# Softmax sums divided out by exp of a negated logarithm instead of a transfer, and the steps of a fused attention and mixture-of-experts kernel laid out anew

## The chip, the cores and the metric

The kernel runs on one core of a Trainium2 chip. The metric is the time of one execution on the device in microseconds, lower is better; the median of three executions is compared. The engines are named as in the profile: PE (TensorE, matmuls; PEld is its weight load), DVE (VectorE), ACT (ScalarE), POOL (GpSimd) and SP (SyncE, which here only issues DMAs).

## The reference

64 batches of 128 tokens with 128 features go through a gated cross-attention over a context of 77 tokens with 96 features per batch, then through a gated mixture of 8 experts of which each token takes the best two. All is float32. Cut to what matters:

```python
q = heads(layernorm(x) @ Wq)            # 16 heads of 8
k, v = heads(ctx @ Wk), heads(ctx @ Wv)
attn = softmax(where(mask, q @ k.T * 8 ** -0.5, -big))
x = x + tanh(g_xattn) * (unheads(attn @ v) @ Wo)

h = layernorm(x)
score, idx = top_k(softmax(h @ Wg), 2)
score = score / (score.sum(-1) + 1e-8)
y_e = (silu(h @ W11[e]) * (h @ W12[e])) @ W2[e]      # I = 256
x = x + tanh(g_ffn) * sum(score[k] * y_idx[k] for k in range(2))
```

## The kernel before

**Attention.** Four batches make a group; there are 16 groups (`G`, `NG`). One loop step `i` handles one batch in a pipeline: `scores` of batch i (four matmuls into the one PSUM tile `sc`, L843; then on DVE the maximum `mx`, L852, and the subtraction in two pieces, `pe` and `pls`, L855), `turn` of batch i-1 (PE turns the weights, `tp` L865, ACT takes the exponential into `pT`, L870), `values` of batch i+2 (`pv`, L818 and L828, then the ACT copy `va`, L834), `mix` of batch i-2 (`po`, L897, then the ACT copy `os`, L904) and `turn_last` of batch i-1 (`tl`, L878). The last product gives two things side by side: with `va` as weights the weighted values, and with `own`, a constant of zeros and ones, the sums of the softmax weights, in the same rows. So the quotient can be formed after `mix`.

`own` repeats each head's sum over the 8 rows of that head, but the sums then have 128 rows for 16 heads. Before, the step `sums` collects 16 rows of each of the four batches with four DMAs (`zc`, 8 KB each), `inverses` takes one DVE reciprocal over 64 x 128 (`rz`, L548) and spreads it back to 128 rows with four DMAs (`rb`, 64 KB each, L551), and `quotients` multiplies (`aT`, L560). `project` (`py`, L569) and `residual` (L575) follow, then the second layer norm and the routing.

**Order of the work.** All steps of a group that are not in the batch pipeline have a place in the table `AT`: `"sums": (6, POST)` puts it at loop step 4g+6, after the pipeline's work; `PRE` puts it ahead. The order of instructions on PE, ACT, DVE and POOL is exactly the order in which the program writes them; on SP the framework's scheduler sets it. Within one step and place, older groups come first. Each engine takes its queue in order, so an instruction that waits holds up all that stand behind it. Three PSUM buffers (`product`) are shared by `tp`, `tl`, `po` and all the steps' products.

**Routing.** For each group DVE finds the best two experts of a token (L629 to L664), POOL adds up counts (`both` L673, `run` L677), PE and DVE turn them to rows (`places`, `dest`), and POOL scatters the rows to a buffer in memory sorted by expert (`xg`, L707): one indirect DMA for each batch and each of the two choices, so eight per group, here as two in each of the four steps `dispatch0` to `dispatch3`, with a memset of one element between. The groups form two parts with a sorted buffer each; part 0 holds the first `SPLIT` = 11 groups. The steps that build the list of tiles (`tiles_*`) run once per part, and `bounds*` writes an empty block behind each expert's rows.

**Experts.** The sorted rows are worked off in tiles of 128, 142 in all, 95 of part 0 and 47 of part 1. A tile is loaded (`xt`), turned (`ptt` L972, `xTt` L974), goes up (`pu` L982, ACT silu L988, DVE product L990), is turned (`phh` L997, `hTt` L999), goes down (`pot` L1005, `y` L1011) and is scattered by POOL into token order (`yb`, L1012), in a pipeline of six further steps. The part of `AT` that lies past the attention loop, `rest`, is spread over the first tiles of part 0 less four. Results of part 0's groups are fetched (`ys`), added to x (`combine`, L1048) and stored, beginning 19 tile steps after part 0's tiles, two steps apart: at steps 114 to 140. The groups of part 1 follow after the last tile. The pool for `ys` has four buffers.

**Layer norm.** Its factor is ln and exp on ACT (`rs_a`, L346), or a power on POOL where `late` is set: before, for the second norm of the last three groups. ACT holds one function table at a time; the attention uses one with both exp and ln, loaded once at the start, while the experts' silu needs another.

Of the kernel before, what the change touches and what calls it, by code (L numbers as in the profile page):

```python
# [8 lines left out]
F32 = mybir.dt.float32  # L9
# [8 lines left out]
HEADS = 16  # L18
HD = 8
# [5 lines left out]
JL = 16  # L25
PRE, POST = 0, 1
TOPK = 2
LATE = 3
RW = 132
PAST = 1 << 20  # L30
LN_EPS = 1e-5
GATE_EPS = 1e-8
SPLIT = 11


@with_exitstack
def tile_gated_xattn_moe(
# [84 lines left out]
    nc.scalar.dma_start(out=wk, in_=Wk)  # L122
    nc.scalar.dma_start(out=wq, in_=Wq)
    nc.scalar.dma_start(out=wv, in_=Wv)
    nc.scalar.dma_start(out=wo_in, in_=Wo)
    nc.scalar.dma_start(out=wg, in_=Wg)
    nc.scalar.dma_start(out=gates[:, 0:1], in_=g_xattn.partition_broadcast(P))
    nc.scalar.dma_start(out=gates[:, 1:2], in_=g_ffn.partition_broadcast(P))
# [131 lines left out]
    nc.gpsimd.memset(own, 0.0)  # L260
    for k in range(2):
        nc.vector.tensor_copy(
            own[:, k, 2 * k : 2 * k + 2], h64.unsqueeze(2).to_broadcast([P, 2, HD])
        )
    nc.vector.tensor_copy(
        own[:, 2:4].rearrange("p u h d -> p (u h) d"),
        h16.rearrange("p u h -> p (u h)").unsqueeze(2).to_broadcast([P, 2 * HQ, HD]),
    )
    iota8 = const.tile([P, E], U32, name="iota8")
    nc.gpsimd.iota(iota8, [[1, E]], base=0, channel_multiplier=0)  # L270

# [3 lines left out]
    czs = [const.tile([CD, G, 3, JL], F32, name=f"czs{i}") for i in range(3)]  # L275
    for t in pls + czs:
        nc.gpsimd.memset(t, 0.0)
    spare_w = const.tile([1, 1], F32, name="spare_w")


    for pt in parts:
# [9 lines left out]
    with ExitStack() as ph:  # L291
# [76 lines left out]
        def transposed(src, n):  # L368
# [5 lines left out]
            nc.scalar.copy(xT, pt)  # L374
            return xT

        AT = {
            "loads": (-22, POST),  # L380
            "stats_a0": (-13, POST),
            "sel_0": (-13, POST),
            "stats_a1": (-9, PRE),
            "sel_1": (-11, PRE),
            "shift_a": (-8, POST),
            "sel_2": (-10, POST),
            "context_t": (-7, PRE),
            "rows_a0": (-8, POST),
            "rows_a1": (-6, PRE),
            "keys": (-2, PRE),  # L390
            "queries_t": (-6, POST),
            "queries": (-4, PRE),
            "sums": (6, POST),
            "inverses": (7, PRE),
            "quotients": (7, POST),
            "project": (8, POST),
            "residual": (8, POST),
            "stats_f0": (9, PRE),
            "stats_f1": (9, POST),
            "shift_f": (11, PRE),  # L400
            "rows_f0": (11, PRE),
            "rows_f1": (12, PRE),
            "rows_f2": (14, PRE),
            "rows_t": (12, POST),
            "logits": (14, PRE),
            "less_max": (14, PRE),
            "gates_exp": (16, PRE),
            "gates": (16, PRE),
            "experts": (16, PRE),
            "counts": (16, PRE),  # L410
            "places": (18, PRE),
            "places_in": (18, PRE),
            "tiles_count": (17, POST),
            "tiles_ends": (17, POST),
            "tiles_list": (18, PRE),
            "tiles_turn": (18, POST),
            "tiles_keep": (19, PRE),
            "dispatch0": (19, PRE),
            "dispatch1": (19, POST),
            "dispatch2": (20, POST),  # L420
            "dispatch3": (21, POST),
            "bounds0": (18, PRE),
            "bounds1": (19, PRE),
            "bounds2": (19, POST),
            "bounds3": (20, POST),
        }
        TURN = {}

# [104 lines left out]
            nc.scalar.copy(gr.qT, pq)  # L533

        @step("sums")
        def sums(gr, g):
            gr.zc = s2.tile([G * HEADS, S], F32, tag="zc", name=f"zc_{g}")
            for b in range(G):  # L540
                nc.sync.dma_start(
                    out=gr.zc[b * HEADS : (b + 1) * HEADS], in_=gr.os[0:P:HD, b, 1]
                )

        @step("inverses")
        def inverses(gr, g):
            rz = s2.tile([G * HEADS, S], F32, tag="rz", name=f"rz_{g}")
            nc.vector.reciprocal(rz, gr.zc)  # L548
            gr.rb = s2.tile([P, G, S], F32, tag="rb", name=f"rb_{g}")
            for b in range(G):  # L550
                nc.sync.dma_start(  # L551
                    out=gr.rb[:, b],
                    in_=rz[b * HEADS : (b + 1) * HEADS].unsqueeze(1)
                    .to_broadcast([HEADS, HD, S]),
                )

        @step("quotients")
        def quotients(gr, g):
            gr.aT = s2.tile([P, T], F32, tag="aT", name=f"aT_{g}")
            nc.vector.tensor_tensor(  # L560
                gr.aT.rearrange("p (b t) -> p b t", b=G), gr.os[:, :, 0], gr.rb, ALU.mult
            )


# [17 lines left out]
        @step("stats_f1")  # L582
        def stats_f1(gr, g):
            gr.ln.stats(2, 4)
            gr.ln.factors(late=g >= NG - LATE)

        @step("shift_f")
        def shift_f(gr, g):
# [112 lines left out]
            nc.vector.tensor_reduce(to, at, AX.X, ALU.add)  # L701
            nc.vector.tensor_copy(gr.dest, to)

        def dispatch(b):
            def f(gr, g):
                for k in range(TOPK):
                    i = nc.gpsimd.indirect_dma_start(  # L707
                        out=part_of(g).xg[:, :],
                        out_offset=bass.IndirectOffsetOnAxis(
                            ap=gr.dest[:, k, b : b + 1], axis=0  # L710
                        ),
                        in_=gr.rows[:, b, k, :],
                        in_offset=None,
                    )
                    apart(i, f"dispatch{part_of(g).c}")
                    nc.gpsimd.memset(spare_w, 0.0)

            return f

        for b in range(G):  # L720
            step(f"dispatch{b}")(dispatch(b))


        def of_part(name):
# [83 lines left out]
        def values(gr, g, b):  # L808


            pvm = pv[:, : 8 * 32].rearrange("p (q k m) -> p q k m", q=NQ, k=2)
            wvm = wv.rearrange("c (q k h d) -> c q k h d", q=NQ, k=2, h=2)
            pvl = pv[:, 8 * 32 : 12 * 32].rearrange("p (f u m) -> p f u m", f=2, u=2)
            wvl = wv.rearrange("c (f u h d) -> c f u h d", f=2, u=2, h=HQ)
            for h in range(2):
                for k in range(2):
                    o = 8 * (2 * k + h)
                    nc.tensor.matmul(  # L818
                        pvm[64 * h : 64 * h + 64, :, k, o : o + HD],
                        gr.cT[:, b, :JM], wvm[:, :, k, h], start=True, stop=True,  # L820
                    )
            cz = gr.cz[:, b].rearrange("c z j -> c (z j)")
            for z in range(2):
                for u in range(2):
                    for hp in range(2):
                        h = 2 * hp + z
                        r = 64 * u + 32 * hp
                        nc.tensor.matmul(  # L828
                            pvl[r : r + 32, :, u, h * HD : h * HD + HD],
                            cz[:, JL * (1 - z) : JL * (1 - z) + 32],  # L830
                            wvl[:, :, u, h], start=True, stop=True,
                        )
            va = a4.tile([P, 12, 32], F32, tag="va", name=f"va_{g}_{b}")
            nc.scalar.copy(va.rearrange("p u m -> p (u m)"), pv[:, : 12 * 32])  # L834
            return va
# [48 lines left out]
                pT[:, 8:10], tp, AF.Exp, bias=drop[:, 1, i : i + 1], scale=scale  # L884
            )

        def mix(b, va, pT, os, n):

            po = product([P, 2, S], f"po_{n}")
            for v in range(2):  # L890
                for c in range(3):
                    for q in range(NQ):
                        if v == 0:
                            w = va[:, 2 * q + c if c < 2 else 8 + q]
                        else:
                            w = own[:, c if c < 2 else 2 + q % 2].rearrange("p h d -> p (h d)")
                        nc.tensor.matmul(  # L897
                            po[32 * q : 32 * q + 32, v, :],
                            w,
                            pT[:, 2 * q + c if c < 2 else 8 + q // 2, :],  # L900
                            start=(c == 0),
                            stop=(c == 2),
                        )
            nc.scalar.copy(os[:, b], po)  # L904

# [10 lines left out]
        for i in range(min(TURN)[0], NBT + 2):  # L918
# [11 lines left out]
            if 0 <= i - 2 < NBT:  # L930
                g, b = divmod(i - 2, G)
                if b == 0:
                    groups[g].os = s3.tile([P, G, 2, S], F32, tag="os", name=f"os_{g}")
                mix(b, vas.pop(i - 2), pTs.pop(i - 2), groups[g].os, f"{g}_{b}")
            if 0 <= i - 1 < NBT:
                turn_last(pTs[i - 1], i - 1)
            advance(i, POST)
        advance(NBT + 2, PRE)
        advance(NBT + 2, POST)
        at_.close()  # L940


        lp = ph.enter_context(tc.tile_pool(name="lp", bufs=26))
# [57 lines left out]
        def down(ti, t):  # L1001
            po = ps_u.tile([P, D], F32, tag="pd", name=f"pot_{t}")
            for c in range(NC):
# [5 lines left out]
                )  # L1009
            y = yp.tile([P, D], F32, tag="y", name=f"y_{t}")  # L1010
            nc.vector.tensor_scalar_mul(y, po, ti.x[:, D + 1 : D + 2])  # L1011
            i = nc.gpsimd.indirect_dma_start(  # L1012
                out=ti.pt.yb[:, :],
                out_offset=bass.IndirectOffsetOnAxis(
# [5 lines left out]
                oob_is_err=False,  # L1020
            )
            apart(i, f"results{ti.pt.c}")
            nc.gpsimd.memset(spare_w, 0.0)


        ts = [Tile(pt, k) for pt in parts for k in range(pt.nt)]
# [89 lines left out]
```

## Time and profile before

| | us |
|---|---|
| three executions | 801.7, 793.98, 795.58 |
| median | 795.58 |
| the profiled execution | 799.03 |
| its span on the profile | 797.3 |
| PE busy | 665.8 (84%) |
| DVE busy | 484.1 (61%) |
| ACT busy | 388.8 (49%) |
| POOL busy | 363.3 (46%) |
| mean granted clock of PE | 0.936 |

The first scores start at about 30 us, the last group leaves the attention loop at about 447, the experts run from 451 to 776, and the last store ends at 797.3. A row of the groups gives the source line, engine, operation, what it writes and reads, and the count, then the busy time in us and the mean of one in ns, then how long the engine stood idle just before and what ended most of that. A row of the waits gives engine and tile waited for, then the total in us, the count, and the longest. A row of the timeline gives start, duration and the instruction, and in brackets how long its engine had been idle, with what released it. "Remote" is a release that the profile does not name.

### The profile page before, as it was taken

The numbers are of one execution on the slowest core, as the hardware profiler recorded it, in microseconds if no ns is written. First come the engines' busy times: TensorE is split into PE (matmuls) and PEld (weight loads), VectorE is DVE, ScalarE is ACT, GpSimd is POOL, SyncE is SP. The second block draws the span as 40 slices with busy tenths as digits, with TensorE's granted clock in tenths as the row PEclk, the third lists the DMA queues.
The fourth block names the chain that finished last, engine by engine and source line by source line (L and its number), as shares of the span: only waits on it lengthen the run. The fifth ranks groups of instructions, "written<-read, shape, count | busy, mean of one in ns | idle before, by whom it ended". The sixth has DMA issues, their size and how long they took to land.

```text
span 797.3 us, 21532 instructions
## 1 busy us (share of the span) xinstructions
PE 665.8 (84%) x7695; PEld 462.5 (58%) x7695; DVE 484.1 (61%) x1452; ACT 388.8 (49%) x960; POOL 363.3 (46%) x774
## 2 busy tenths in 40 slices
PE   2999999988998989887988758888788678998880
PEld 2577776766676666666656436555555445665450
DVE  4467888777877877775668434544444434556653
ACT  3577877656665667664554333234334223342230
POOL 4211113455345445543225435665666576565451
PEclk9999999999999999997989879898999899999995
DMA  6671111111111110110121342222222212446626
GB/s 155 180 186 28 28 23 36 35 47 38 46 35 48 33 36 28 38 37 19 34 57 34 71 92 60 65 69 58 67 76 62 78 55 71 115 153 195 173 68 202
DMA packets 75753, 58.40 MB, mean 73 GB/s; under 512 B 16075, under 2 KB 69471, under 8 KB 75648
## 3 DMA queue, kind: packets, MB, share of 16 engines
q1 hardware_dynamic: 57088, 35.27, 18.3%
q0 software_dynamic: 8640, 17.06, 6.6%
q10 hardware_dynamic: 9920, 4.69, 2.1%
q8 instruction: 63, 1.03, 0.5%
q14 instruction: 42, 0.34, 0.1%
HBM read 28.98 MB, written 24.20 MB: 67 GB/s over the span
## 4 chain that ended last, share of the span: by engine, by line
PE 71%; DVE 8%; issue 7%; DMA 4%; SPq 3%; ACT 3%; another core or an unknown queue 3%; POOL 1%; ACTq 0%; POOLq 0%; DVEq 0%
PE pu L982 15%; PE po L897 11%; PE tp L865 8%; PE pot L1005 7%; PE sc L843 6%; PE phh L997 4%; PE ptt L972 3%; PE tl L878 2%; PE pv L818 2%; PE py L569 2%; PE pq L531 2%; PE pg L622 2%; PE pv L828 2%; DMA rb<-rz 1%
## 5 line engine op out<-in xcount | busy, mean ns | idle before, releaser
L1012 POOL DMA_INDIRECT yb<-y,xt x142 | 140.7, 991 | 130.4 <-DVE xTt L974 69.3
L707 POOL DMA_INDIRECT xg<-rows,dest x128 | 125.1, 977 | 90.3 <-DVE gm L629 60.7
L982 PE MATMUL pu<-wx,xTt 128*128 x284 | 158.5, 641 | 7.8 <-issue 6.7
L988 ACT ACTIVATE sgt<-pu 128x256 f32<-128x256 f32 x142 | 54.5, 384 | 196.0 <-PE pu L982 122.3
L990 DVE TENSOR_TENSOR ht<-sgt,pu 128x256 f32<-128x256 f32 x142 | 59.6, 420 | 117.1 <-ACT sgt L988 65.9
L852 DVE TENSOR_REDUCE mx<-sc 128x16 f32<-128x1232 f32 x64 | 91.9, 1435 | 39.2 <-PE sc L843 35.2
L997 PEld LDWEIGHTS phh<-ident,ht 128*128 128x128 f32 x284 | 40.2, 146 | 94.7 <-issue 76.1
L870 ACT ACTIVATE pT<-tp,drop 128x512 f32<-128x512 f32 x128 | 82.0, 685 | 24.9 <-PE tp L865 16.9
L1005 PE MATMUL pot<-wx,hTt 128*128 x568 | 90.3, 284 | 0.1
L865 PEld LDWEIGHTS tp<-ident,pe 128*128 128x128 f32 x512 | 61.7, 153 | 32.8 <-issue 15.8
L865 PE MATMUL tp<-ident,pe 128*128 128x128 f32 x512 | 78.7, 302 | 2.0 <-ACT kb L520 1.3
L855 DVE TENSOR_TENSOR pe<-sc,mx 128x1024 f32<-128x1024 f32 x64 | 78.4, 1225 | 2.2
L1005 PEld LDWEIGHTS pot<-wx,hTt 128*128 128x128 f32 x568 | 78.3, 200 | 0.2 <-issue 0.2
L897 PE MATMUL po<-pT,own 128*32 128x128 f32 x1536 | 66.4, 278 | 10.7 <-issue 10.7
L972 PE MATMUL ptt<-ident,xt 128*128 128x128 f32 x142 | 42.7, 300 | 35.6 <-DVE xTt L974 22.1
L1011 DVE TENSOR_SCALAR y<-pot,xt 128x128 f32<-128x128 f32 x142 | 49.3, 347 | 31.8 <-remote 10.9
L997 PE MATMUL phh<-ident,ht 128*128 128x128 f32 x284 | 57.1, 284 | 12.5 <-ACT hTt L999 8.4
L897 PE MATMUL po<-pT,va 128*32 128x128 f32 x1536 | 61.5, 279 | 4.8 <-issue 4.1
L843 PE MATMUL sc<-kb,qT 32*128 32x308 f32 x512 | 59.0, 525 | 3.8 <-DVE pls L855 3.1
L999 ACT COPY hTt<-phh 128x256 f32<-128x256 f32 x142 | 52.3, 368 | 14.9 <-PE pu L982 8.6
L897 PEld LDWEIGHTS po<-pT,own 128*32 128x32 f32 x1536 | 48.2, 112 | 18.3 <-issue 17.9
L834 ACT COPY va<-pv 128x384 f32<-128x384 f32 x64 | 30.9, 483 | 53.5 <-PE po L897 23.3
(161 smaller groups left out, 1037.7 us busy)
## 6 DMA issues: line engine op xcount, KB each, us to landing
xt<-xg SPq DMA_DIRECT2D x142, 66.0 KB
ys<-yb SPq DMA_DIRECT2D x16, 512.0 KB
rb<-rz SPq DMA_DIRECT2D x64, 64.0 KB
out_dram<-x ACTq DMA_DIRECT2D x16, 256.0 KB
x<-in_x_dram SPq DMA_DIRECT2D x15, 256.0 KB
yb<-y,xt POOLq DMA_INDIRECT x142
wx<-in_L_ffn_W_dram SPq DMA_DIRECT2D x2, 1024.0 KB
xg<-rows,dest POOLq DMA_INDIRECT x128
```

The source lines that it names most:

```text
L707: i = nc.gpsimd.indirect_dma_start(out=part_of(g).xg[:, :], out_offset=bass.IndirectOffsetOnAxis(ap=gr.dest[:, k, b : b + 1], axis=0), in_ ...
L843: nc.tensor.matmul(sc[:, q, :W], gr.qT[r, b * S : (b + 1) * S], gr.kb[r, b].rearrange("p h j -> p (h j)"), start=True, stop=True,)
L852: nc.vector.tensor_reduce(mx[:, :, :, 0], sv, AX.X, ALU.max)
L855: nc.vector.tensor_tensor(dst[:, :, :, : j1 - j0], sv[:, :, :, j0:j1], mx.to_broadcast([P, NQ, HQ, j1 - j0]), ALU.subtract,)
L865: nc.tensor.transpose(tp[:, u, :], pe[:, q + u // 2, 2 * (u % 2) : 2 * (u % 2) + 2].rearrange("p h j -> p (h j)"), ident,)
L870: nc.scalar.activation(pT[:, 2 * q : 2 * q + 4], tp, AF.Exp, bias=drop[:, 0, i : i + 1], scale=scale)
L897: nc.tensor.matmul(po[32 * q : 32 * q + 32, v, :], w, pT[:, 2 * q + c if c < 2 else 8 + q // 2, :], start=(c == 0), stop=(c == 2),)
L972: nc.tensor.transpose(pt, ti.x[:, :D], ident)
L982: nc.tensor.matmul(pu.rearrange("p j i -> p (j i)"), ti.xT, wxf[:, bass.ds(ti.e, 2 * I)], start=True, stop=True,)
L997: nc.tensor.transpose(pt[:, c], ti.h[:, c], ident)
L1005: nc.tensor.matmul(po, ti.hT[:, c], wxf[:, bass.ds(ti.e + w, D)], start=(c == 0), stop=(c == NC - 1),)
L1012: i = nc.gpsimd.indirect_dma_start(out=ti.pt.yb[:, :], out_offset=bass.IndirectOffsetOnAxis(ap=ti.x[:, D : D + 1].bitcast(I32), axis=0), i ...
```

## The change

- `sums` and its transfers go. `mix` copies only the values to `os`, and ACT takes the logarithm of the sums into `lz`. `inverses` becomes one exponential of -`lz` on ACT, in place over the group's 128 x 512, and `quotients` multiplies by `lz`.
- In `values`, four tiles of 32 columns at 64 moving columns take the place of tiles of 64 columns at 32. The order of the heads inside 32 rows changes; `own` and the rows of `Wo` follow it, `Wo` now loaded in eight DMAs of 16 rows on ACT's queue.
- `dispatch` becomes eight steps of one scatter. The memset of `spare_w`, now 128 x 1, stands ahead of each scatter, also of the result scatters.
- `SPLIT` is 12: part 0 has 103 tiles, part 1 has 39; results of part 0 are fetched from step 122.
- `late` is true only after the attention loop, which is group 15.
- `AT` is laid out anew.

```diff
-SPLIT = 11
+SPLIT = 12
...
-    nc.scalar.dma_start(out=wo_in, in_=Wo)
+    for q in range(NQ):
+        for k in range(2):
+            r = 32 * q + 16 * k
+            nc.scalar.dma_start(
+                out=wo_in[r : r + 16], in_=Wo[32 * q + 16 * (1 - k) : 32 * q + 16 * (2 - k)]
+            )
...
-            "loads": (-22, POST),
-            "stats_a0": (-13, POST),  "sel_0": (-13, POST),  "stats_a1": (-9, PRE),
-            "sel_1": (-11, PRE),  "shift_a": (-8, POST),  "sel_2": (-10, POST),
-            "context_t": (-7, PRE),  "rows_a0": (-8, POST),  "rows_a1": (-6, PRE),
-            "keys": (-2, PRE),  "queries_t": (-6, POST),  "queries": (-4, PRE),
-            "sums": (6, POST),  "inverses": (7, PRE),  "quotients": (7, POST),
-            "project": (8, POST),  "residual": (8, POST),  "stats_f0": (9, PRE),
-            "stats_f1": (9, POST),  "shift_f": (11, PRE),  "rows_f0": (11, PRE),
-            "rows_f1": (12, PRE),  "rows_f2": (14, PRE),  "rows_t": (12, POST),
-            "logits": (14, PRE),  "less_max": (14, PRE),  "gates_exp": (16, PRE),
-            "gates": (16, PRE),  "experts": (16, PRE),  "counts": (16, PRE),
-            "places": (18, PRE),  "places_in": (18, PRE),
-            "dispatch0": (19, PRE),  "dispatch1": (19, POST),
-            "dispatch2": (20, POST),  "dispatch3": (21, POST),
+            "loads": (-15, PRE),
+            "stats_a0": (-14, PRE),  "sel_0": (-14, PRE),  "stats_a1": (-10, PRE),
+            "sel_1": (-13, PRE),  "shift_a": (-9, POST),  "sel_2": (-11, POST),
+            "context_t": (-7, POST),  "rows_a0": (-9, POST),  "rows_a1": (-8, PRE),
+            "keys": (-4, POST),  "queries_t": (-7, POST),  "queries": (-5, PRE),
+            "inverses": (6, PRE),  "quotients": (6, POST),
+            "project": (7, POST),  "residual": (7, POST),  "stats_f0": (8, POST),
+            "stats_f1": (9, PRE),  "shift_f": (10, PRE),  "rows_f0": (10, PRE),
+            "rows_f1": (11, PRE),  "rows_f2": (11, PRE),  "rows_t": (11, POST),
+            "logits": (13, PRE),  "less_max": (13, PRE),  "gates_exp": (14, PRE),
+            "gates": (15, PRE),  "experts": (15, PRE),  "counts": (15, PRE),
+            "places": (17, PRE),  "places_in": (17, PRE),
+            "dispatch00": (17, POST),  "dispatch01": (17, POST),
+            "dispatch10": (18, PRE),  "dispatch11": (18, POST),
+            "dispatch20": (19, PRE),  "dispatch21": (19, POST),
+            "dispatch30": (19, POST),  "dispatch31": (20, POST),
...
-            rz = s2.tile([G * HEADS, S], F32, tag="rz", name=f"rz_{g}")
-            nc.vector.reciprocal(rz, gr.zc)
-            gr.rb = s2.tile([P, G, S], F32, tag="rb", name=f"rb_{g}")
-            for b in range(G):
-                nc.sync.dma_start(
-                    out=gr.rb[:, b],
-                    in_=rz[b * HEADS : (b + 1) * HEADS].unsqueeze(1)
-                    .to_broadcast([HEADS, HD, S]),
-                )
+            nc.scalar.activation(gr.lz, gr.lz, AF.Exp, scale=-1.0)
...
-            gr.ln.factors(late=g >= NG - LATE)
+            gr.ln.factors(late=after[0])
...
-        def dispatch(b):
+        def dispatch(b, k):
             def f(gr, g):
-                for k in range(TOPK):
-                    i = nc.gpsimd.indirect_dma_start(
+                nc.gpsimd.memset(spare_w, 0.0)
+                i = nc.gpsimd.indirect_dma_start(
...
             for h in range(2):
-                for k in range(2):
-                    o = 8 * (2 * k + h)
+                for j in range(2):
+                    r = 64 * h + 32 * j
                     nc.tensor.matmul(
-                        pvm[64 * h : 64 * h + 64, :, k, o : o + HD],
-                        gr.cT[:, b, :JM], wvm[:, :, k, h], start=True, stop=True,
+                        pvm[r : r + 32, :, 1:3, HD * h : HD * h + HD],
+                        gr.cT[:, b, 32 * j : 32 * j + 32], wvm[:, :, :, h],
+                        start=True, stop=True,
                     )
...
-            nc.scalar.copy(os[:, b], po)
+            nc.scalar.copy(gr.os[:, b], po[:, 0])
+            nc.scalar.activation(gr.lz[:, b], po[:, 1], AF.Ln)
```

In the table the lines are joined three to a row here; steps of the tile lists, which run once per part, are left out.

## The prediction

> **What bounds the kernel now.** I read the slices first (19.9 us each), then the groups, the waits, windows cut by stage, and the timeline around the waits that mattered.
>
> ```profile
> PE   2999999988998989887988758888788678998880
> DVE  4467888777877877775668434544444434556653
> PEclk9999999999999999997989879898999899999995
> ```
>
> PE is nearly full wherever its clock digit is 9, but not packed: attention (slices 1 to 22) holds nines and eights, the experts after it more gaps. DVE comes second at 0.7 to 0.8 in attention, so a gain on PE there can run into DVE.
>
> ```profile
> L852 DVE TENSOR_REDUCE mx<-sc 128x16 f32<-128x1232 f32 x64 | 91.9, 1435 | 39.2 <-PE sc L843 35.2
> L904 ACT COPY os<-po 128x256 f32<-128x256 f32 x64 | 24.0, 375 | 33.1 <-remote 8.8 <-PE pt_f L372 8.3 <-PE po L897 7.5
> L818 PE MATMUL pv<-wv,cT 96*64 96x32 f32 x512 | 29.2, 236 | 0.0
> L548 DVE RECIPROCAL rz<-zc 64x128 f32<-64x128 f32 x16 | 15.0, 937 | 0.0
> L560 DVE TENSOR_TENSOR aT<-os,rb 128x512 f32<-128x512 f32 x16 | 12.8, 799 | 35.5 <-DMA rb<-rz 33.3 <-issue 2.2
> ```
>
> The last row is what the change aims at: DVE stands 33.3 us before the quotients (aT) for the transfer that spreads the reciprocals. The waits give it 15 times and one long one:
>
> ```profile
> DVE aT L560 <- DMA rb<-rz: 33.3, 15, 8.3
> DVE x L575 <- PE py L569: 25.1, 10, 6.3
> ```
>
> Windows (busy of PE, PEld, DVE, ACT, POOL, then the clock): a steady stretch of attention, one at full clock, the two groups that scatter four at a time, the long wait, steady experts.
>
> ```profile
> 200.00:240.00 40.00, 37.17 (x605) 27.48 (x607) 31.28 (x87) 26.90 (x65) 17.04 (x38) 0.91 0.14 38
> 304.00:329.00 25.00, 23.02 (x417) 16.96 (x415) 20.45 (x62) 17.65 (x43) 13.10 (x30) 1.00 0.15 36
> 355.00:389.00 34.00, 28.09 (x447) 21.07 (x447) 18.90 (x53) 18.12 (x42) 10.39 (x25) 0.85 0.11 26
> 466.00:476.00 10.00, 1.10 (x8) 0.71 (x6) 1.36 (x4) 3.55 (x5) 2.50 (x6) 0.69 0.39 86
> 680.00:720.00 40.00, 38.94 (x208) 25.45 (x206) 21.65 (x73) 15.03 (x46) 24.40 (x48) 1.00 0.46 133
> ```
>
> PE lacks 2.8 us of 40 in steady attention, 8.9 of 10 in the fourth window. In the third, the timeline shows four scatters in a row and, a microsecond after the last, ACT and PE taking up work long due:
>
> ```profile
> 355.79 0.98 POOL L707 DMA_INDIRECT xg<-rows,dest  x1 [0.15 <-issue]
> ...
> 359.62 0.97 POOL L707 DMA_INDIRECT xg<-rows,dest  x1 [0.23 <-issue]
> 361.64 0.37 ACT L904 COPY os<-po 128x256 f32<-128x256 f32 x1 [3.99 <-remote]
> 362.07 1.23 PE L569 MATMUL py<-wo,aT 128*128 128x128 f32 x4 [4.52 <-ACT os L904]
> ```
>
> Pairs of scatters do it for about 2.3 us (scatters 159.94 to 162.21, no signal from PE 160.7 to 162.95). The Trainium skill ("SBUF — State Buffer", section "SBUF: two separate sides") says that only the port pair shared by VectorE and GpSimd causes contention, and that PE and ACT never wait there. By that rule no spacing of the scatters changes PE's time and the two rivals below that rest on it have no chance; the 4.52 us above speak against it.
>
> **The change part by part,** against the profiled execution: span 797.3, and 1.73 around it, 799.03, which is 3.45 above the median of 795.58.
>
> *Start: +2.5 (0 to +6).* wo comes as 8 DMAs on ACT's queue for 1: seven more issues of 0.42 to 0.52 us, 3.3 in all, ahead of wg and the gates (landed 9.5, then the tanh at 9.54). The eight pieces also land ahead of DVE's copy to wo (11.08), behind which stand the first-context row (11.36) and POOL's selection (11.65). The next bound, kr landing at 13.49, covers some 1.3. That leaves about 2; the eighth own copy on DVE adds a few tenths. Nothing covers it beyond: lower end 0, upper 6 if each piece lands later too.
>
> *The wait for rb in attention: -13 (0 to -25).* Gone are sums (4 DMAs of 8 KB), inverses (4 of 64 KB) and 25.0 of the 33.3 us, 1.7 to 2 per group. A wait on DVE counts only as far as PE runs dry: PE idles 2.8 of 40 us, some 30 over attention. Half is taken. What is late next is residual, which waits for py already (25.1).
>
> *Layout: -14 (0 to -28).* A transition from one step to the next takes, by the starts of the maxima (L852), the longer of PE's 4.2 plus its extra steps and DVE's 3.03 (1.435 + 1.225 + 0.366) plus its extras. Adding each group's steps at their offsets by their row durations gives 6.7, 6.8, 6.7, 5.2, together 25.4 us, before; measured groups take 24.5 (304 to 329, full clock) to 27.4. The new offsets, without the 937 ns reciprocal, give 6.7, 5.6, 5.8, 6.0, 24.1. So 1.3 for the 11 groups whose transitions carry all three stages, 14. Zero if ACT or the three PSUM buffers set the pace instead; -28 if the measured 27.4 falls by twice as much.
>
> *Values: -5 (0 to -7.7).* The eight instructions of L818 take 0.43 us per step and start in pairs, 59 ns apart. With four tiles side by side they should start as po's do (four within 20 ns, 109 ns per four at 128 columns, half that at 64), 0.12 less, 7.7 over 64 steps. PE is not always the bound, so -5. The own and wo orders change no count of instructions.
>
> *ACT: +4 (0 to +28).* A copy of 128x256 (375 ns) becomes a copy of 128x128, by the rows of 256, 384 and 512 columns (375, 483, 595) 0.265, and a logarithm. That is not in the trace: between the copy, 0.265, and the 128x128 activation with scale and bias, 0.490; by the exps of 256 and 512 columns (477, 685) 0.37. So 0.26 more, 64 times, 16.8, and 16 exps of 128x512 at 0.685, 11.0: 27.8 of busy ACT, most under ACT's idle third (26.9 of 40). Unhidden is some of the later release of PSUM; all if ACT becomes the bound. No table loads stand in attention, where ln and exp already run in turn for rs_a, so the new ones add none. The skill ("ScalarE: Activation LUTs", section "What ACT_TABLE_LOAD costs") gives an activation with immediate scale and bias 186 ns plus 0.833 per element, by which the logarithm would be an estimated 293 ns and the 27.8 would be 22.9. No run so far shows it; the term stays.
>
> *Experts: -8 and -2.6.* The last group's rb transfers queue on SP behind 14 tile loads:
>
> ```profile
> 470.52 2.55 SPq L551 DMA_DIRECT2D rb<-rz  x4
> 474.98 0.69 DVE L560 TENSOR_TENSOR aT<-os,rb 128x512 f32<-128x512 f32 x1 [8.25 <-DMA rb<-rz]
> 475.93 0.47 PE L972 MATMUL ptt<-ident,xt 128*128 128x128 f32 x1 [8.90 <-DVE xTt L974]
> ```
>
> Without them 8 of PE's 8.90 go (0 to -8.9; the exp that comes instead waits for nothing but ACT). One more group finishes its gates within attention, so one exp and one silu table load (1.283 each) go: -2.6 (0 to -2.6).
>
> *Scatters: 0 (-30 to +49).* Of each group's eight, four pairs become runs of 3, 2 and 1, and 2, and after attention's last loads runs of 3 and 5; the experts see 25 for 32. Moving them past POOL's own steps leaves POOL's sum as it is. Fewer seams, but longer: I take 0.
>
> *The rest: 0.* Loads move from 22 steps ahead to 15, past SP's waits for sums and inverses, which are gone; all x loads were issued by about 40 us, attention runs to 447, so the later place costs nothing unless SP holds them back, then a step (4.4 to 8.3) or two at the first groups. The memsets between scatters, 88 ns, now fill 128 partitions and stand ahead; POOL at 17 of 40 covers that, and the result scatters at the very end, 1.27 each, do not: 10 of them by at most 0.09. The factors of groups 13 and 14 go from POOL's pow to ACT's ln and exp, the longer stay on ACT inside the +4.
>
> *End: -3.3 (0 to -7).* Combines slow the tiles they fall among: 4.62 us for two tiles from 717 to 765 against 2 x 1.63 in the last window above, 1.36 each. All 11 fall among tiles (steps 117 to 137 of 142); of the 12 at 125 to 147 about three fall past the last tile: two fewer, -2.7, and one that now lies bare, +1.4. Five groups after the last scatter become four, which fit the four buffers: the fifth's wait (0.62) and combine (1.42) go, -2.0.
>
> Sum: 2.5 - 13 - 14 - 5 + 4 - 8 - 2.6 + 0 - 3.3 = -39.4. 799.03 - 39.4 = 759.6; less 3.45, 756.
>
> **Rivals.**
>
> *A, the attention gain is hidden:* DVE's waits were not PE's, and ACT's 27.8 and py's wait take their place. For it: DVE at 31 of 40 and x's 25.1. Against: PE has 2.8 of 40 to win. Only values' -5 stays of attention: 2.5 - 5 - 8 - 2.6 - 3.3 = -16.4, giving 779.
>
> *B, the scatters stop pairing:* single scatters halt nothing. Experts before have 16 pairs, attention the rest; the 25 left in the experts stand singly beside result scatters. 16 pairs at 1.3 of the 2.3 us is 21 more: 735. For it: single result scatters every 1.63 us in the last window leave PE 38.94 of 40. Against: runs of two and three stay in attention.
>
> *C, slower: the longer runs halt PE.* Place: rows, sel and dispatch steps, POOL's runs of 3 and 5. Price: from 355 to 419 groups took 33.8 and 29.9 where 27.4 is usual, 4.5 each beyond; in 11 groups 49, less the 39.4: +10, 805. It decides from 3.6 us per group on (39.4 / 11). Against: at 145 to 285 pairs are the rule already, and a run of 3 replaces a pair and a half.
>
> **How the numbers follow.** Forecast 0.42 (756, own range 738 to 774), A 0.22, B 0.14, C 0.22. The measurement tells about 1% from no change, 787.6 to 803.5. Faster: all of the forecast and B, A but for 0.03, 0.01 of C: 0.76. Same: 0.03 of A and 0.08 of C, 0.11. Slower: 0.13. From 730 to 805 leaves out half of C (0.11) and a third of B (0.05).
>
> **What would show it.** Right: no DVE wait at aT beyond 1 us, no gap of 8 us on PE near 470; groups of about 24 by the maxima; L818's rows starting four together; ACT at 31 of 40 and still waiting for PE; no more than two silu-exp switches; four ys loads at the end. Wrong: groups at 27 with DVE waiting for py (A), or PE silent for 3 us and more after runs of 3 and 5 scatters (C), with clock digits of 8 behind them.

## The result, and the profile after

The changed kernel takes 750.85 us, the median of four runs (747.86 to 757.1), against 794.78 of the kernel before in the same comparison: a ratio of 0.948 (95% interval 0.938 to 0.958). Forecast was 756, range 730 to 805. The profiled execution spans 755.4 against 797.3. Cut by the starts of the maxima (L849 after, L852 before) and of the tiles (`xTt`):

| stretch | before | after | difference |
|---|---|---|---|
| start to 1st maximum | 31.2 | 31.9 | +0.7 |
| 1st to 17th (groups 0 to 3) | 84.8 | 78.2 | -6.6 |
| 17th to 52nd (steady groups) | 230.7 | 203.6 | -27.1 |
| 52nd to 64th (last groups) | 88.5 | 97.1 | +8.6 |
| 64th to the first tile | 15.8 | 18.5 | +2.7 |
| tile 0 to 117 | 265.2 | 250.2 | -15.0 |
| tile 117 to 141 | 53.3 | 48.7 | -4.6 |
| to the end | 27.8 | 27.2 | -0.6 |
| span | 797.3 | 755.4 | -41.9 |

The total is near the forecast, its parts are not: the steady groups gain more than was expected of them, the last groups lose. The slices of the page (18.9 us each) show it:

```profile
PE   2899999999999999788887489888888887999880
DVE  4468798878788787644577245444443543455674
PEclk9999999999999999977798689999999999999995
```

PE's nines now run to slice 16 and the clock's to slice 17; before, PE's eights began in slice 9. Then come three slices at clock 7, in the last groups of attention, and a PE slice of 4 at the passage to the experts. DVE falls with it, to 4 to 7 in the last groups and 2 at the passage, so it isn't DVE that binds there. The groups that the change put in, from the full list of groups:

```profile
L813 PE MATMUL pv<-wv,cT 96*32 96x64 f32 x512 | 21.3, 240 | 0.0
L902 ACT ACTIVATE lz<-po 128x128 f32<-128x128 f32 x64 | 18.5, 289 | 0.0
L550 ACT ACTIVATE lz<-lz 128x512 f32<-128x512 f32 x16 | 9.9, 618 | 0.0
L555 DVE TENSOR_TENSOR aT<-os,lz 128x512 f32<-128x512 f32 x16 | 11.3, 706 | 7.7 <-ACT lz L550 7.7
L901 ACT COPY os<-po 128x128 f32<-128x128 f32 x64 | 17.3, 270 | 27.4 <-remote 13.9 <-PE po L894 9.9 <-PE sc L840 1.9
```

DVE waits at aT once now, 7.7 us, in place of 33.3 over 15 times. The windows (busy of PE, PEld, DVE, ACT, POOL, clock) give the steady stretch, the last groups and the passage:

```profile
200.00:280.00 80.00, 76.11 (x1367) 56.59 (x1365) 65.21 (x197) 61.93 (x161) 43.37 (x93) 1.00 0.10 32
314.00:411.00 97.00, 77.71 (x1194) 56.99 (x1196) 54.94 (x166) 49.22 (x120) 31.17 (x72) 0.82 0.08 24
411.00:430.00 19.00, 9.15 (x158) 7.32 (x146) 7.24 (x22) 7.25 (x19) 9.83 (x22) 0.80 0.13 40
```

PE goes from 95% at full clock to 80% at 0.82. The timeline shows the last run of five scatters:

```profile
419.30 0.84 PE L894 MATMUL po<-pT,own 128*32 128x128 f32 x24
420.53 0.97 POOL L702 DMA_INDIRECT xg<-rows,dest  x1 [0.19 <-issue]
...
424.55 0.95 POOL L702 DMA_INDIRECT xg<-rows,dest  x1 [0.19 <-issue]
426.49 0.27 ACT L901 COPY os<-po 128x128 f32<-128x128 f32 x1 [5.81 <-remote]
427.89 0.61 ACT L550 ACTIVATE lz<-lz 128x512 f32<-128x512 f32 x1
428.86 0.45 PE L972 MATMUL ptt<-ident,xt 128*128 128x128 f32 x1 [8.73 <-DMA xt<-xg]
```

By the profile, which models the ends of matmuls, PE had finished po at 420.14; ACT takes it up at 426.49, a microsecond after the last of the five scatters ends at 425.50. It looks as if a run of scatters holds up what PE reports to the other engines, its signals; whether PE reports late or ends late, the profile can't tell. The stall of 8.90 near 470 is gone, and one of 8.7 has come here.

### The profile page after: what moved, and what is told of

It reads as the page before. It is cut to its first block, busy times and chain, and to the rows that moved or that the text cites. A ratio compares the mean times of both kernels' runs of the same rounds, so it can differ in the third digit from the quotient of the medians.

```text
span 755.4 us, 21356 instructions
## 1 busy us (share of the span) xinstructions
PE 639.6 (85%) x7695; PEld 444.6 (59%) x7695; DVE 464.4 (61%) x1437; ACT 393.2 (52%) x1042; POOL 368.2 (49%) x770
## 4 chain that ended last, share of the span: by engine, by line
PE 73%; issue 6%; DVE 6%; another core or an unknown queue 4%; DMA 4%; ACT 3%; POOL 3%; SPq 0%; POOLq 0%; ACTq 0%; DVEq 0%
PE pu L982 16%; PE po L894 13%; PE tp L862 8%; PE pot L1005 7%; PE sc L840 7%; PE phh L997 4%; PE tl L875 3%; PE ptt L972 3%; PE pq L543 2%; PE py L564 2%; PE pv L813 2%; PE pg L617 2%; POOL yb L1013 1%; PE pt_a L379 1%
## 5 line engine op out<-in xcount | busy, mean ns | idle before, releaser
L982 PE MATMUL pu<-wx,xTt 128*128 x284 | 155.7, 631 | 7.3 <-issue 6.7
L849 DVE TENSOR_REDUCE mx<-sc 128x16 f32<-128x1232 f32 x64 | 91.7, 1432 | 45.8 <-PE sc L840 45.2
L894 PE MATMUL po<-pT,va 128*32 128x128 f32 x1536 | 68.9, 277 | 14.6 <-issue 12.0
L852 DVE TENSOR_TENSOR pe<-sc,mx 128x1024 f32<-128x1024 f32 x64 | 78.3, 1224 | 2.2
L862 PEld LDWEIGHTS tp<-ident,pe 128*128 128x128 f32 x512 | 58.7, 148 | 30.6 <-issue 12.2
L862 PE MATMUL tp<-ident,pe 128*128 128x128 f32 x512 | 74.4, 291 | 1.2 <-ACT lz L902 0.8
L894 PE MATMUL po<-pT,own 128*32 128x128 f32 x1536 | 61.4, 279 | 3.6 <-issue 3.6
L894 PEld LDWEIGHTS po<-pT,va 128*32 128x32 f32 x1536 | 42.6, 111 | 25.6 <-issue 25.2
L840 PE MATMUL sc<-kb,qT 32*128 32x308 f32 x512 | 56.1, 510 | 1.4 <-DVE pls L852 1.3
L355 POOL TENSOR_TENSOR rs_a<-rs_a,live 128x4 f32<-128x4 f32 x16 | 3.2, 199 | 108.3 <-ACT rs_a L353 104.0
```

The source lines that it names most:

```text
L840: nc.tensor.matmul(sc[:, q, :W], gr.qT[r, b * S : (b + 1) * S], gr.kb[r, b].rearrange("p h j -> p (h j)"), start=True, stop=True,)
L849: nc.vector.tensor_reduce(mx[:, :, :, 0], sv, AX.X, ALU.max)
L852: nc.vector.tensor_tensor(dst[:, :, :, : j1 - j0], sv[:, :, :, j0:j1], mx.to_broadcast([P, NQ, HQ, j1 - j0]), ALU.subtract,)
L862: nc.tensor.transpose(tp[:, u, :], pe[:, q + u // 2, 2 * (u % 2) : 2 * (u % 2) + 2].rearrange("p h j -> p (h j)"), ident,)
L894: nc.tensor.matmul(po[32 * q : 32 * q + 32, v, :], w, pT[:, 2 * q + c if c < 2 else 8 + q // 2, :], start=(c == 0), stop=(c == 2),)
L982: nc.tensor.matmul(pu.rearrange("p j i -> p (j i)"), ti.xT, wxf[:, bass.ds(ti.e, 2 * I)], start=True, stop=True,)
```

## Experiments

Theory at the outset: the steady groups gained because DVE no longer waits for the transfers, and the last groups lost to runs of scatters. The rival: DVE's wait was never PE's, and it is scatters everywhere. The first four kernels and the next four ran in sets in which the kernel before took 788.2 and 786.7; the last four in a set in which it took 700.3, on the same chip as the second set, so those are compared by ratio and among themselves only. Where kernels of different sets are set against each other, the set is a part of the difference that no run here separates. Stretches are those of the table above.

**ln and exp alone, in the kernel before.**

```diff
-            nc.scalar.copy(os[:, b], po)
+            nc.scalar.copy(gr.os[:, b], po[:, 0])
+            nc.scalar.activation(gr.lz[:, b], po[:, 1], AF.Ln)
...
-            "sums": (6, POST),
...
+            nc.scalar.activation(gr.lz, gr.lz, AF.Exp, scale=-1.0)
```

> The kernel before with one part of the change alone: the sums are inverted by ln and exp on ACT, at the places that inverses and quotients had; the transfers are gone. Theory (the terms of the forecast: -13 in attention, +4 for ACT, -8 for the wait near 470 us): about 17 us below the kernel before, 778 against 795, with half of it near 470. Rival A (DVE's wait in attention hid nothing): only the 8 us, 787. If instead the transfers held up more than PE's idle time shows (the steady groups' whole gain of some 4 us per group is theirs): 740 to 750.

755.69, ratio 0.960 (0.953 to 0.968): 32 us gained, twice the forecast's terms. The steady groups fall from 27.4 to 23.6 us each, the whole stretch by 25.8, tiles 0 to 117 by 7.5; the stretches add up to more than 32 because the profiled execution of the kernel before, 799.03, lies 10.9 above this set's median. PE's clock, 0.94 in 200 to 280 before, is 1.00:

```profile
200.00:280.00 80.00, 76.04 (x1345) 57.12 (x1338) 65.48 (x203) 59.50 (x158) 44.60 (x97) 1.00 0.10 31
```

**The old layout in the changed kernel.**

```diff
-            "inverses": (6, PRE),
-            "quotients": (6, POST),
-            "dispatch00": (17, POST),
-            "dispatch01": (17, POST),
...
+            "inverses": (7, PRE),
+            "quotients": (7, POST),
+            "dispatch00": (19, PRE),
+            "dispatch01": (19, PRE),
...
```

> The changed kernel with the order of steps of the kernel before (scatters two by two at the four old places), all else as changed. Theory (layout was worth 14 us): 765 against 751 of the changed kernel. If the layout carries the whole gain of the steady groups (33.7 us up to the 52nd maximum): about 785, less the 11 us that its longer scatter runs lose at the end of attention, 774. If the layout is worth nothing: 751.

746.77, ratio 0.946 (0.938 to 0.955), and 0.948 (0.938 to 0.958) for the changed kernel in the first comparison: with the old layout it is as fast as with the new. Steady stretch 204.3 against 203.6; last groups 82.2 against 97.1; first maximum 34.3 against 31.9; tiles 0 to 117 255.6 against 250.2.

**A pause between scatters.**

```diff
-                nc.gpsimd.memset(spare_w, 0.0)
+                nc.gpsimd.memset(gap_w, 0.0)
```

> The changed kernel with a longer pause between scatters: the memset ahead of each scatter of the routing is 128 x 512, all else as changed. Theory (back-to-back scatters hold up PE's signals, and the runs of 3 and 5 at the end of attention cost 8 to 11 us): the pause lets signals through, 740 to 744. Rival (the scatters have nothing to do with it, as the port rule says, and the last groups are slow for want of other work): 751 or, by POOL's added work in the experts' pace, up to 5 more.

The memset is 128 x 512 and takes 0.54 us for 0.11. 714.11, ratio 0.908 (0.901 to 0.916), further than the theory went. Last groups 66.1 for 97.1, passage 12.6 for 18.5, tiles 0 to 117 241.2 for 250.2; the steady stretch is 4.3 longer, at 207.9. That is the clock's: in each of eight steady groups PE now waits some 0.65 us at `pp` (L681), in five of them 3.4 us at a granted clock of 0.50 follow, and these five take 24.3 to 24.4, the other three 22.9 to 23.1. At the passage ACT takes the copy os in the middle of the run of scatters, 0.67 us after po ends, where it had been 6.35:

```profile
390.60 0.84 PE L895 MATMUL po<-pT,own 128*32 128x128 f32 x24
392.11 0.27 ACT L902 COPY os<-po 128x128 f32<-128x128 f32 x1
```

PE's busy time in the same window as above is up from 77.71, the clock from 0.82:

```profile
314.00:411.00 97.00, 86.33 (x1403) 62.61 (x1402) 72.93 (x245) 60.85 (x157) 62.96 (x112) 0.96 0.17 48
```

**Eight scatters in one place.**

```diff
-            "dispatch00": (17, POST),
+            "dispatch00": (18, POST),
...
-            "dispatch31": (20, POST),
+            "dispatch31": (18, POST),
```

> The changed kernel with all eight scatters of a group in one place, at 18 steps after the group's first, all else as changed: runs of about 10 us. Theory (a run holds up PE's signals from its second scatter to its end, and PE can go on for two to three us without them): some 5 to 7 us lost in each of the 12 to 13 groups that scatter in attention, 810 to 840. Rival (scatters do not touch PE): 751, within 5 us.

815.07, ratio 1.036 (1.028 to 1.044). Steady groups take 30.8 for 23.2, 7.6 more where the theory had 5 to 7. The timeline of PE inside one run (213.37 to 223.25) shows that PE itself comes to crawl:

```profile
219.08 0.30 PE L894 MATMUL po<-pT,va 128*32 128x128 f32 x2 [1.13 <-issue]
219.77 0.96 POOL L702 DMA_INDIRECT xg<-rows,dest  x1 [0.19 <-issue]
220.48 1.10 PE L894 MATMUL po<-pT,va 128*32 128x128 f32 x4 [1.09 <-issue]
221.03 0.96 POOL L702 DMA_INDIRECT xg<-rows,dest  x1 [0.19 <-issue]
221.92 0.43 PE L894 MATMUL po<-pT,va 128*32 128x128 f32 x2 [0.34 <-issue]
```

A few matmuls to a scatter, with "issue" before them: PE waits for nothing that the profile names.

**The pause in the kernel before.** The same edit as above, on the kernel before.

> The kernel before, transfers and layout and all, with the memset between the scatters of the routing made 128 x 512 (0.54 us for 0.09). Theory S (PE's 1.6 to 1.8 us of idle time per steady group, and the half clock that follows it, come from a pair of scatters that holds up the signal for the copy of po; the transfers' wait alone costs little): steady groups fall from 27.4 to about 24, the end of attention and the experts gain as they did in the changed kernel, 730 to 740. Theory W (the wait for rb makes PE idle, scatters only lengthen the end): steady groups stay at 26 to 27, about 755.

753.33, ratio 0.954 (0.945 to 0.963). The total is theory W's; the steady groups take about 25.1, in between, and the waits still have

```profile
DVE aT L561 <- DMA rb<-rz: 28.0, 13, 7.0
```

so DVE waits nearly as long as before, while PE's gaps of 1.6 to 1.9 us at py are gone (0.6 is the longest wait left there), and with them the half clock, but for one stretch of 3.4 us at 174. PE's idle time goes as theory S has it:

```profile
200.00:280.00 80.00, 74.77 (x1296) 55.16 (x1294) 65.15 (x185) 56.85 (x138) 52.53 (x90) 1.00 0.16 41
```

**The transfers kept, their wait taken away.**

```diff
-            "quotients": (7, POST),
-            "project": (8, POST),
-            "residual": (8, POST),
+            "quotients": (8, POST),
+            "project": (9, PRE),
+            "residual": (9, PRE),
```

> The kernel before with the transfers kept, but quotients a step later (8, after the pipeline's work), project and residual at 9 ahead of it, so that the transfers have landed when DVE comes to the quotients. Theory W (the wait for rb makes PE idle): the wait and PE's 1.6 us go, and the clock with them, steady groups at 23.6 to 24.5 and some 30 us less than before. Theory S (a scatter pair on the copy of po does it): the wait at aT goes, but steady groups keep 26 to 27 unless the shift moves scatter and copy apart; within 10 us of the kernel before.

797.5, ratio 1.013 (1.009 to 1.017). The wait for rb is gone from the waits, and nothing is gained: the steady groups take 26 to 29. PE still stands at py, for 2.1 us:

```profile
248.49 0.98 POOL L707 DMA_INDIRECT xg<-rows,dest  x1 [0.15 <-issue]
249.78 0.96 POOL L707 DMA_INDIRECT xg<-rows,dest  x1 [0.21 <-issue]
251.43 0.37 ACT L904 COPY os<-po 128x256 f32<-128x256 f32 x1 [1.12 <-PE pt_f L372]
252.35 0.91 PE L569 MATMUL py<-wo,aT 128*128 128x128 f32 x6 [2.10 <-ACT pT L883]
```

The first theory falls here. In the kernel before it is the same pair at the same place, from 195.02 to 197.27, and behind it the copy os, which empties one of the three shared PSUM buffers:

```profile
197.96 0.37 ACT L904 COPY os<-po 128x256 f32<-128x256 f32 x1 [1.88 <-PE pt_f L372]
198.38 1.16 PE L569 MATMUL py<-wo,aT 128*128 128x128 f32 x8 [1.81 <-ACT os L904]
```

With ln and exp the pair comes just behind the copy:

```profile
206.67 0.27 ACT L887 COPY os<-po 128x128 f32<-128x128 f32 x1
206.77 0.99 POOL L690 DMA_INDIRECT xg<-rows,dest  x1 [0.15 <-issue]
207.24 1.08 PE L552 MATMUL py<-wo,aT 128*128 128x128 f32 x8
```

**The old layout with the pause.** Both edits above, on the changed kernel.

> The changed kernel with the order of steps of the kernel before, and with the long pause between scatters. Theory (the layout's own worth is nothing, PE at full clock sets the pace in both; what differs between layouts is where scatters fall): equal to the changed kernel with the pause, 714, within 5. If the forecast's 1.3 us per group is there once the scatters are out of the way: 728.

734.17, ratio 0.931 (0.925 to 0.936), against 0.908 (0.901 to 0.916) for the new layout with the pause, from another set: once scatters are apart the new layout seems to be worth some 2%, if the sets are alike. Neither expectation has it: it does not lie in the steady groups (22.9 to 24.4 in both). Tiles 0 to 117 take 255.3 against 241.2, the last groups and the passage 86.7 against 78.7, but the profiled execution here took 740.28, 6 above the median, so where the 2% lies isn't shown.

**The old values with the pause.**

```diff
-                for j in range(2):
-                    r = 64 * h + 32 * j
+                for k in range(2):
+                    o = 8 * (2 * k + h)
...
+    nc.scalar.dma_start(out=wo_in, in_=Wo)
```

> The changed kernel with the long pause between scatters, and with values, own and the load of Wo as before (one DMA). Forecast's terms: values +5, start -2.5, so 716 to 717 against 714. If values lie beside other work and only the start counts: 711. If the whole 0.12 us per step is on the path: 719.

718.6, ratio 0.914 (0.908 to 0.920), against 0.908 (0.901 to 0.916): not told apart. The steady stretch is the same, 208.0 and 207.9. The first maximum comes at 28.7 for 32.1, but the 17th at 111.5 for 108.4.

**Eleven groups in the first part, with the pause.**

```diff
-SPLIT = 12
+SPLIT = 11
```

> The changed kernel with the long pause between scatters (714) and 11 groups in the first part instead of 12. Forecast's term for the end: 3.3 us slower, 717. By the stages of the kernels so far (tiles 117 to 141 took 53.6 with 11 and 48.8 with 12, the tail the same within 1): 4 to 5 slower, 719. If the combines lie beside other work: 714.

665.73, ratio 0.949 (0.945 to 0.953). Tiles 117 to 141 take 53.4, and 48.6 in the next kernel, as expected. But the two totals lie 15.3 apart, 9.7 of it in tiles 0 to 117 (216.9 and 207.2), which no expectation had; the steady stretch, where they differ in the pause, is 182.6 in both.

**The pause for the late groups alone.**

```diff
+                nc.gpsimd.memset(gap_w if g >= 9 else spare_w, 0.0)
```

> The changed kernel with the long pause for the scatters of groups 9 to 15 alone, the short one for groups 0 to 8. Theory (only the runs at the end of attention and in the experts cost; in the steady groups the long pause holds up POOL's counts and costs the 4.3 us that the stage shows, 207.9 against 203.6): 709 to 710. Rival (pairs and runs of three cost in the steady groups as much as the pause): 714.

650.42, ratio 0.930 (0.925 to 0.934), the fastest of its set. Its steady groups take 20.8, but so do those of the kernel with 11 groups and the long pause everywhere: in this set the steady groups lose nothing to either, so the 4.3 of the theory is not there, and its totals, made for another set, can't be judged. In code the steady groups are the changed kernel's, where they took 23.2. After a pair ACT takes the copy va without idling here (199.28); in the changed kernel's profile it idled 2.05 us for it (212.97), while po came in pieces. The experts are quicker too: tiles 0 to 117 take 207.2, and 241.2 with the pause everywhere in the first set. What set this set apart isn't shown; it was the chip of the second set.

**Eight in one place, with the pause.**

```diff
-                nc.gpsimd.memset(spare_w, 0.0)
+                nc.gpsimd.memset(gap_w, 0.0)
```

> The changed kernel with all eight scatters of a group in one place, and the long pause ahead of each, so POOL is bound for 13.6 us instead of 10. Theory (what halts PE is scatters that follow one another within 0.3 us, and a pause lets its signals through): steady groups fall from 30.8 to 23 to 25, 720 to 740. Rival (the block of POOL's queue makes the others wait, whatever stands between): 815 or more.

The eight stand at (18, POST) as in the experiment without the pause. 719.48, ratio 1.027 (1.023 to 1.032): a miss for the theory, whose steady groups were 23 to 25 and are 27.2. That the time lies near its 720 is chance, as the kernel before is 11% faster in this set. PE works through the run without "issue" gaps, but then waits for POOL's counts, which stand behind the eight:

```profile
215.27 0.97 POOL L703 DMA_INDIRECT xg<-rows,dest  x1 [0.16 <-issue]
216.26 0.26 POOL L669 TENSOR_TENSOR both<-took 128x32 f32<-128x32 f32 x1
216.57 0.41 PE L681 MATMUL pp<-both,earlier 128*128 128x32 f32 x2 [2.92 <-POOL both L669]
```

Once in each group, 2.92 and 0.43 us, and then 6.8 us at half clock, which is 3.4 more: 6.75 together, where its groups (27.2) exceed the 20.8 by 6.4. So POOL's longer queue costs PE 6.4 us per group here. Whether the pause is what let PE through can't be said: in this set pairs without a pause cost nothing either, and eight without one were not run in it.

**ln and exp alone, with the pause.** The first experiment with the pause.

> The kernel before with ln and exp alone in place of the transfers, and the long pause between scatters: to be set against the kernel before with the pause (753, steady groups 25.1). Forecast's terms (-13 + 4 in attention, -8 for the stall near 470 us): 736. If with the scatters out of the way DVE's wait for the transfers hides nothing of PE's: only the 8, 745. If the transfers cost as much as in the bare comparison (32 us): 721.

681.84, ratio 0.972 (0.968 to 0.976). Its set lacks a kernel with transfers and pause, so the terms can't be read from it. Against the kernel before it gains 18.4 us with both parts, where either alone gained 32 and 33 in the slower sets. Its steady groups take 22.2 against 20.8 with the new layout and values.

## Why the prediction was right, and where it was not

That the time lay 5 us from the forecast is luck: errors of both signs met. Of the signs that it named, those of rival C came beside its own: steady groups of 23.2 and no gap of 8 us near 470, but also a copy that ACT waits 5.81 us for behind a run of five scatters, with clock digits of 6 and 7.

*The wait for rb, -13, with ACT's +4.* Of the right sign, far too small, for the wrong reason. ln and exp alone gave 32 us, 35.6 of attention's stretches (404.0 to 368.4 between first and last maximum), 7.5 of the experts'. The step that failed: "A wait on DVE counts only as far as PE runs dry: PE idles 2.8 of 40 us". The idle time was put down to DVE's wait because both recurred once a group. But taking the wait away while the transfers stayed gave nothing, and keeping it while parting the scatters took the idle time away. PE stood at py because a pair of scatters held back the copy os, and six of seven such gaps of 1.6 to 1.9 us in the steady groups were followed by 3.4 us at half clock, 1.7 more, which the forecast did not price. Of the 3.8 us per group, 2.3 go when the scatters are parted (27.4 to 25.1). The other 1.5 (25.1 to 23.6) would be the transfers' own, about twice the 0.8 that 13 over 16 groups means; but the two kernels ran in different sets, and no run shows it alone. That the pair came free of the copy is a shift of a microsecond or so and was in no sum. ACT was costed well, if high: ln 0.289 against 0.37 taken, copy 0.270 against 0.265, exp 0.618 against 0.685; ACT 30.4 of 40. The 0.293 worked out from the Trainium skill ("ScalarE: Activation LUTs", section "What ACT_TABLE_LOAD costs") was nearer than the rows of other shapes.

*Layout, -14.* Next to nothing in the steady groups: 23.7 with the old places, 23.2 with the new, where the rule gave 25.4 and 24.1. Both measured times lie below the rule's sums, and 20.8 was reached in the last set, so extra steps hide beside other work more than adding their rows allows. In that set 22.2 against 20.8 is of the forecast's size, though values are in that too. With the pause the layout may be worth 2%; without it the runs of scatters take it back: +14.9 in the last groups against the old places.

*Scatters, 0, and rival C.* In the steady groups runs of three cost no more than the old pairs (23.2 against 23.7). The runs of five did what C says, at its place, for three groups instead of eleven: 29.1, 34.7 and 30.2 against 23.5, 26.6 and 29.7 with the old places. C's price of 4.5 was of the size of these (5.6, 8.1, 0.5), its number of groups was not; so it did not decide. B's 21 us are in reach: 9.0 of the experts' time and 31.0 of the last groups' went with the pause.

*The port rule.* The Trainium skill ("SBUF — State Buffer", section "SBUF: two separate sides") has PE never waiting there. PE's data may not; but a pause of 0.43 us more on POOL took the kernel from 0.948 to 0.908 of before. Which resource holds up the signals no run shows, so the rule as to ports is not refuted; that no spacing changes PE's time is.

*Values, -5.* L813 fell to 21.3 us from 29.2 of L818, and the steady groups did not move (208.0, 207.9). *Start, +2.5.* The gates came 2.8 later and wo 3.1 (14.17 for 11.08), as priced, and with the old places it shows (34.3 for 31.2); with the new +0.7 is left. That firstT now goes ahead of wo on DVE, so that the first context product comes at 12.99 for 15.26, is no reason for the difference: with the old places it does so too, and the product comes at 13.26. What the new places save at the start stays open. *Experts, -10.6.* -15.0 to tile 117, of which 7.5 came with ln and exp alone; the rest isn't assigned, though part 0 of 12 groups instead of 11 goes with 9.7 less there in the last set. Two silu-exp switches for three as forecast; the 8.9 us stall shrank to 3.0 there and moved to the passage in the changed kernel. *End, -3.3.* -5.2: tiles 117 to 141 4.6, the tail 0.6.

## What to carry to other kernels

That one engine waits in the same microseconds as another idles is no proof: before pricing a wait, ask what the trace shows if it goes while its work stays. In two of the three sets here indirect scatters back to back delayed what PE's partners learn from it until the run ended; part them by a short instruction, but keep POOL's own results, that others wait for, out from behind them. A gap on PE of 1.6 us cost twice where the clock fell after it, and in some groups the clock fell after one of 0.65.

## Not expected of the hardware

In a run of eight scatters ACT idled up to 8.93 us before it could take the copy va, and PE's own matmuls came a few to a scatter. With 0.54 us in place of 0.1 between scatters, in runs of up to five, PE's results came through at once. And the kernel before took 700 us in one set and 787 in another; a steady group of the same code 20.8 and 23.2, at the same granted clock of 1.00. Why PE's signals were held up less in one set, on the same chip, stays open.
